# GNN preparation on one core: x asked for first, half of the normalising and the moments' sums on GpSimd, one edge step at a time

## The chip, the core and the metric

The kernel runs on one core of one Trainium2 chip. The metric is the device time of one execution in microseconds (us), and the time of a kernel is the median of several runs. Profiled executions give a span (first to last instruction) and, a little longer, the execution's own time. Engines are named as in the profile: PE is TensorE's matmul, PEld its weight load, DVE is VectorE, ACT is ScalarE, POOL is GpSimd, and SP is SyncE, which here only issues DMAs.

## What is computed

x is 6250 nodes by 256 channels; src and dst hold 100,000 edges, sorted by dst. The reference normalises x, runs three layers and a head, and adds the result to x:

```
h = relu(layernorm(x))
for l in 0..2:  h = relu((h + agg(h)) @ W1[l] + b1[l]);  h = relu(h @ W2[l] + b2[l]);  h = h @ W3[l] + b3[l]
h = relu((h + agg(h)) @ cW1 + cb1);  h = relu(h @ cW2 + cb2);  out = x + h @ cW3 + cb3
agg(h)[n] = sum of h[src[e]] over the edges e with dst[e] = n
```

## The kernel before

The nodes are 49 tiles of 128 rows. Since agg is linear, the kernel multiplies by W1 first: the table of layer 0 is relu(layernorm(x)) @ W1[0], and a later layer's W3 is folded into the next W1. Most of agg is done as dense products with a count matrix of the graph, built on the chip from the edges; for the other tiles (`gone`) rows are gathered from the table by indirect DMA.

All this runs inside `tc.manual_schedule()`: each engine's instructions stand in the order in which the program issues them, so an instruction that waits holds everything behind it on its engine. The preparation (line 1147 on) interleaves three generators, and each `next` issues a stage of one of them:

- `rows = normed(...)` (L1009) makes table 0 and its two halves in `XY` (a rounded high part, L1103, and the rest, L1108). It works on 25 pairs of tiles; step s of its loop issues, each for another pair: `out` (the product's copy from PSUM, L1092, pair s-3), `high` (L1103, s-4), `scale` (normalise and relu, L1061, pair s), `turn` (four transposes on PE, L1070, and the copy back from PSUM, L1073, s-1), `times` (eight products with W1, L1082, s-2), `moments` (statistics, L1035, s+4, and, when a group of tiles is full, four small operations on DVE and a square root on ACT, L1041 to L1047), `low` (L1108, s-4) and `keep` (the store of four tiles to the table, s-5). `settle` (L1053) makes the scale and shift that `scale` reads. x comes in groups of six tiles (`load`, four buffers), the first group in two parts.
- `looked = look(...)` (L653) treats the edges: it loads dst (`run`) and src (`srcs`), stores two rearranged copies of them in DRAM (`split_d`, `ends_d`), finds by comparing (L785 to L813: one subtraction, three Sign passes on ACT, two compares and a reduction on DVE) where each stretch of nodes begins, asks for windows of edges by indirect DMA, turns them on PE (L892) into `clT`, from which the graph is later built, and makes the lists `idx` and `rel` for the gathers (L974 to L993).
- `ahead_w = fused(...)` (L576) turns W3 (L590) and multiplies it by the next W1 (L598), once per layer, four stages each; the biases, loaded by `load_biases` (L550) and turned on PE (L567), go into the product too.

`ask(n)` (L643) issues up to n of the waiting indirect requests on POOL. Each is tied to the newest product of `times` (`after`, L632). The driver, before:

```
STAGES = (0, 1, 2, 3, 4, 5, 6, 7, 8, 9, 10, 14, 15, 16, 17, 18, 19, 20, 21, 22, 23, 24, 25, 26, 28)
for i in range(len(range(0, NT, 2)) + 5):
    if i >= 2:
        next(ahead_w, None)
    next(rows)
    ask(2)
    if i in STAGES:
        next(looked, None)
```

Ahead of this loop the driver issues, in order: the first two tiles of x; the small load of first destinations; the rest of the first group, W1 and tiles 6 to 11; dst and src; the six bias rows, the first W3 and W1; the first moments. Step 1 of the loop asks for tiles 12 to 23. After the loop the three generators are run out. The memory of the preparation's pools is then used again: the graph build's first cast (`pairs`, L1220, on ACT) takes its place, and from there on the code is that of the layers.

## Time and profile before

| what | us |
|---|---|
| median of 3 runs | 2042.28 (2041.14 to 2042.76) |
| profiled execution, its own time | 2041.49 |
| its span | 2039.3 |
| PE busy | 1985.8 |
| POOL busy | 1376.4 |
| DVE busy | 909.8 |
| ACT busy | 850.9 |
| first `pairs` cast (L1220) starts | 105.40 |

The page gives one profiled execution. The chain of waits is followed back from the last instruction to what released each step. In a timeline row stand the start, the duration, the engine, the line of the kernel, the operation with its tiles, how many, and in brackets the idle time before it with what ended it. A row of the stretches gives each engine's busy time and number of instructions in a window, then PE's granted clock (1.00 is full), the DMA engines' busy share and GB/s. A row of the groups gives busy time and the mean of one in ns. "SPq" and "ACTq" are DMA issues of those engines' queues.

### The profile page before, as it was taken

How to read it: one execution, taken by the hardware profiler on the slowest of the kernel's cores; microseconds unless marked ns; L12 is line 12 of the kernel's file. 1: busy time of each engine (PE TensorE's matmuls, PEld its weight loads, DVE VectorE, ACT ScalarE, POOL GpSimd, SP SyncE). 2: the span in 40 equal slices, each digit the busy share in tenths (PEclk: the TensorE clock that was granted, in tenths of full speed). 3: DMA queues.
4: the chain of work that ended last, by engine and by line, in shares of the span. 5: the costliest groups of instructions: out<-in, count | busy, mean ns of one | idle time of the engine just before them, and what ended most of it. 6: DMA issues, size and time to landing. Idle time of an engine off the chain costs nothing.

```text
span 2039.3 us, 32998 instructions
## 1 busy us (share of the span) xinstructions
PE 1985.8 (97%) x12075; PEld 1469.4 (72%) x12075; DVE 909.8 (45%) x2080; ACT 850.9 (42%) x1743; POOL 1376.4 (67%) x1452
## 2 busy tenths in 40 slices
PE   5999999999999999999999999999999999999997
PEld 4866766666766877777777777777777777777774
DVE  6788776777672422222333322222233432333333
ACT  5776655556565533232243323223323433233331
POOL 1557777777773577777676577777777477777774
PEclk9999999999999999999999999999999999999999
DMA  6644555555454755455556554555556555655553
GB/s 210 187 143 147 161 153 157 157 159 154 151 157 151 252 165 153 154 173 166 152 178 201 184 167 145 185 159 170 152 184 208 181 189 156 208 192 184 175 175 117
DMA packets 184774, 347.21 MB, mean 170 GB/s; under 512 B 31544, under 2 KB 119098, under 8 KB 184604
## 3 DMA queue, kind: packets, MB, share of 16 engines
q0 software_dynamic: 67440, 183.10, 31.1%
q1 hardware_dynamic: 116632, 160.07, 23.7%
q8 instruction: 96, 1.57, 0.3%
q10 hardware_dynamic: 532, 1.86, 0.3%
q14 instruction: 74, 0.61, 0.1%
HBM read 286.05 MB, written 58.87 MB: 169 GB/s over the span
## 4 chain that ended last, share of the span: by engine, by line
PE 91%; DVE 4%; DMA 2%; ACT 1%; issue 1%; POOL 0%; SPq 0%; ACTq 0%; DVEq 0%; POOLq 0%
PE agg L1945 46%; PE agg L1862 13%; PE sums L1679 11%; PE ps L1503 6%; PE ps L1440 6%; PE bp L1263 4%; PE ps L1745 1%; DVE hi L1225 1%; DVE at L1273 1%; PE bp L1082 1%; DVE lo L1225 1%; PE ps L1432 1%; PE ps L1452 1%; DMA srcs<-in_src_dram 0%; DMA xs<-in_x_dram 0%
## 5 line engine op out<-in xcount | busy, mean ns | idle before, releaser
L1618 POOL DMA_INDIRECT rows<-table,idx x1352 | 1312.3, 971 | 572.2 <-issue 217.1
L1945 PE MATMUL agg<-a,XY 128*128 128x512 f32 x4116 | 978.2, 395 | 2.0 <-DMA table<-zz 2.0
L1945 PEld LDWEIGHTS agg<-a,XY 128*128 128x128 f32 x4116 | 765.7, 188 | 192.6 <-issue 34.7
L1838 ACT CAST a<-at 128x512 fp32r<-128x512 uint8 (+1 forms) x529 | 320.8, 617 | 590.6 <-PE agg L1945 562.7
L1838 DVE CAST a<-at 128x512 fp32r<-128x512 uint8 x528 | 239.8, 456 | 480.8 <-PE agg L1945 463.9
L1862 PE MATMUL agg<-XY,a 128*128 128x512 f32 x1323 | 369.3, 410 | 1.4 <-DVE un L1874 0.7
L1862 PEld LDWEIGHTS agg<-XY,a 128*128 128x128 f32 x1323 | 230.9, 189 | 42.0 <-issue 5.0
L1679 PE MATMUL sums<-rows,hot 128*32 128x256 f32 x3724 | 242.3, 381 | 4.4 <-DMA rows<-table,idx 4.4
L1679 PEld LDWEIGHTS sums<-rows,hot 128*32 128x32 f32 x3724 | 122.4, 110 | 116.4 <-issue 29.3
L1271 ACT CAST at<-bp 128x392 uint8<-128x392 f32 x250 | 120.8, 489 | 188.2 <-PE bp L1263 187.6
L1822 ACT CAST a<-at 128x512 fp32r<-128x512 uint8 (+2 forms) x349 | 191.3, 574 | 7.8 <-PE agg L1862 7.3
L1273 DVE CAST at<-bp 128x392 uint8<-128x392 f32 x230 | 128.7, 559 | 129.5 <-PE bp L1263 129.3
L1703 DVE TENSOR_TENSOR sums<-sums,XY 128x256 f32<-128x256 f32 x85 | 36.5, 430 | 295.0 <-PE agg L1945 277.0
L1225 DVE TENSOR_TENSOR hi<-cols,pairs 128x784 bf16<-128x784 bf16 x240 | 133.8, 558 | 0.0
L1503 PE MATMUL ps<-w,h 128*128 128x256 f32 x588 | 133.5, 379 | 0.0
L1440 PE MATMUL ps<-h,w 128*128 128x512 f32 (+3 forms) x328 | 133.1, 548 | 0.3 <-ACT h L1958 0.3
L1263 PE MATMUL bp<-hi,lo 128*128 128x196 bf16 x960 | 124.4, 250 | 8.8 <-DVE hi L1225 8.1
L1263 PEld LDWEIGHTS <-lo 128*128 128x128 bf16 x960 | 70.1, 98 | 77.7 <-DVE hi L1225 29.0
L1503 PEld LDWEIGHTS ps<-w,h 128*128 128x128 f32 x588 | 111.4, 190 | 16.4
L1749 ACT ACTIVATE h<-ps,bias 128x256 f32<-128x256 f32 (+1 forms) x118 | 47.8, 461 | 155.4 <-PE ps L1745 155.4
L1225 DVE TENSOR_TENSOR lo<-lanes,pairs 128x512 bf16<-128x512 bf16 x240 | 99.2, 413 | 0.8 <-ACT pairs L1220 0.8
L1440 PEld LDWEIGHTS ps<-h,w 128*128 128x128 f32 x328 | 59.9, 189 | 54.0 <-issue 43.1
(213 smaller groups left out, 1011.3 us busy)
## 6 DMA issues: line engine op xcount, KB each, us to landing
at<-mat SPq DMA_DIRECT2D x149, 448.0 KB
mat<-at SPq DMA_DIRECT2D x30, 784.0 KB
rows<-table,idx POOLq DMA_INDIRECT x1352
table<-zz SPq DMA_DIRECT2D x71, 256.0 KB
back<-table SPq DMA_DIRECT2D x109, 128.0 KB
table<-zs SPq DMA_DIRECT2D x12, 512.0 KB
out_dram<-zz SPq DMA_DIRECT2D x23, 256.0 KB
xt<-in_x_dram SPq DMA_DIRECT2D x22, 256.0 KB
```

Of the source, the lines that this page charges most:

```text
L1225: nc.vector.tensor_tensor(o.rearrange("p q (n t) -> p q n t", t=2), values.rearrange("p (n t) -> p n t", t=2)[:, None, :, :].to_broadcast( ...
L1263: mm = nc.tensor.matmul(bp[:, m * HW:(m + 1) * HW], lo[:, q + m, :], hi[:, q + m, :], start=True, stop=True)
L1271: nc.scalar.copy(o, v)
L1273: nc.vector.tensor_copy(o, v)
L1440: mm = nc.tensor.matmul(ps[:mp, :w], weights[l][0][:, c, i * P:i * P + mp], h1[:, c, :w], start=(c == 0), stop=(c == KC - 1))
L1503: mm = nc.tensor.matmul(o, h2[0][:, c, nodes], w3[:, c, :], start=(c == 0), stop=(c == KC - 1))
L1618: got = nc.gpsimd.indirect_dma_start(out=t, out_offset=None, in_=tables[self.l][:, :], in_offset=bass.IndirectOffsetOnAxis(ap=at, axis=0),)
L1679: nc.tensor.matmul(self.sums[m * Q:(m + 1) * Q, :C], self.hot[:, c - min(rounds), m, :], self.shared[over_of[b + i]] if k == T else self.r ...
L1822: nc.scalar.copy(a[:, i * m * P:(i + 1) * m * P].rearrange("p (j d) -> p j d", j=m), counts[b][:, j:j + m, :])
L1838: cast(o, at[:, :, d:d + m * P])
L1862: mm = nc.tensor.matmul(agg, a[:, d:d + P], XY[:, j, :], start=(j == 0), stop=(j == NT - 1))
L1945: mm = nc.tensor.matmul(agg[c][:, :w], XY[:, j, o:o + P], a[:, :w], start=(at == 0 and half == 0), stop=(at == NT - 1 and half == 1))
```

## The change

- x: tiles 12 to 17 are asked for with tiles 6 to 11, ahead of dst and src; tiles 18 to 23 stay at step 1.
- Biases: no longer a tile of their own but rows in the memory of `clT`, set to zero by POOL before the loop, loaded at step 5 together with the first W3 and W1, and turned within the first fused product. The fused products start at step 10 of the loop instead of 2, and the next W1 is asked for one stage later.
- `scale`: the first tile of a pair on ACT, the second on POOL, without relu; the relu is in the turned copy. Three buffers for `h` instead of two, and `turn`, `times`, `out`, `high`, `low` and `keep` each one step later. The five operations of the moments' sums are on POOL, as are the small operations on the counts (`less` to `begin_size`).
- `out`: every second pair on ACT instead of every third, the last two on DVE, and these store at once.
- `look`: the stages are arranged anew. The comparing comes first and the rearranging of the edges is shared out over stages between its passes; the check of the order (`down`) is two stages, the last windows, the gathers' lists and the small checks change places. The loop has 31 steps instead of 30, asks for three requests a step instead of two, and gives `looked` 21 stages in it instead of 25.

The diff, cut to its core:

```diff
-    def load_biases(pool):
+    def load_biases():
...
         nc.gpsimd.memset(rows, 0.0)
-        r = 0
...
-            r += n
+        def bring():
+            r = 0
+            for ap in (b1s, cb1, b2s, b3s, cb2):
+                n, c = ap.shape if len(ap.shape) == 2 else (1, ap.shape[0])
+                flat = ap if len(ap.shape) == 2 else ap.rearrange("(o c) -> o c", o=1)
+                for c0 in range(0, max(c, P), c):
+                    nc.sync.dma_start(out=rows[r:r + n, c0:c0 + c], in_=flat)
...
-        turn()()
...
             shut()
+            if l == 0:
+                turn()()
             open_copies.append(times(KC, l, box))
-            w1 = right_of(l + 1)
             yield
             shut()
+            w1 = right_of(l + 1)
...
-        nc.vector.tensor_scalar(chunk[:R], srcs[:R], 7, None, op0=OP.arith_shift_right)
-        nc.vector.scalar_tensor_tensor(split[:R, :, 0], run[:R, :EC], float(STEP), chunk[:R],
-                                       op0=OP.mult, op1=OP.add)
-        nc.vector.scalar_tensor_tensor(split[:R, :, 1], chunk[:R], float(-P), srcs[:R],
-                                       op0=OP.mult, op1=OP.add)
-        store(split_d, split, REST)
...
-        node = pool.tile([P, GSUB, NSUB - S0], F32, name="chunk", bufs=1)
-        nc.gpsimd.iota(node, pattern=[[STEP * GD, GSUB], [STEP * 64, NSUB - S0]],
-                       base=STEP * 64 * S0, channel_multiplier=0,
-                       allow_small_or_imprecise_dtypes=True)
-        yield
-        ends = pool.tile([P, EC, 2], I32, name="split", bufs=2)
-        nc.scalar.copy(ends[:R, :, 0], run[:R, :EC])
-        yield
-        nc.scalar.copy(ends[:R, :, 1], srcs[:R])
-        store(ends_d, ends, REST + P)
-        yield
...
-        sign(0)
-        yield
-        for i, (g0, g1) in enumerate(((0, 9), (9, GSUB + 1))):
+        def compare(g0, g1):
             shape = [NSUB, g1 - g0, NEAR // FINE]
...
+        sign(0)
+        yield
+        ends = pool.tile([P, EC, 2], I32, name="split", bufs=2)
+        nc.vector.tensor_scalar(chunk[:R], srcs[:R], 7, None, op0=OP.arith_shift_right)
+        nc.vector.scalar_tensor_tensor(split[:R, :, 0], run[:R, :EC], float(STEP), chunk[:R],
+                                       op0=OP.mult, op1=OP.add)
+        nc.scalar.copy(ends[:R, :, 0], run[:R, :EC])
+        yield
+        nc.vector.scalar_tensor_tensor(split[:R, :, 1], chunk[:R], float(-P), srcs[:R],
+                                       op0=OP.mult, op1=OP.add)
+        nc.scalar.copy(ends[:R, :, 1], srcs[:R])
+        yield
+        store(split_d, split, REST)
+        compare(0, 9)
+        sign(1)
+        store(ends_d, ends, REST + P)
+        node = pool.tile([P, GSUB, NSUB - S0], F32, name="chunk", bufs=1)
+        nc.gpsimd.iota(node, pattern=[[STEP * GD, GSUB], [STEP * 64, NSUB - S0]],
+                       base=STEP * 64 * S0, channel_multiplier=0,
+                       allow_small_or_imprecise_dtypes=True)
+        yield
+        compare(9, GSUB + 1)
+        sign(2)
+        yield
...
-        nc.vector.tensor_scalar(less[:NSUB], less[:NSUB], -0.5, float(NEAR // 2), op0=OP.mult,
+        nc.gpsimd.tensor_scalar(less[:NSUB], less[:NSUB], -0.5, float(NEAR // 2), op0=OP.mult,
                                 op1=OP.add)
-        nc.vector.tensor_scalar(first[:NSUB], less[:NSUB], at[:NSUB, 0:1], None, op0=OP.add)
+        nc.gpsimd.tensor_scalar(first[:NSUB], less[:NSUB], at[:NSUB, 0:1], None, op0=OP.add)
...
-        nc.vector.tensor_tensor(more[:NSUB], both[:NSUB, 5:6], both[:NSUB, 4:5], OP.subtract)
-        nc.vector.scalar_tensor_tensor(both[:NSUB, 4:5], more[:NSUB], even[:NSUB, 0:1],
-                                       both[:NSUB, 4:5], op0=OP.mult, op1=OP.add)
+        nc.gpsimd.tensor_tensor(more[:NSUB], both[:NSUB, 5:6], both[:NSUB, 4:5], OP.subtract)
+        nc.gpsimd.tensor_scalar(more[:NSUB], more[:NSUB], even[:NSUB, 0:1], both[:NSUB, 4:5],
+                                op0=OP.mult, op1=OP.add)
+        nc.gpsimd.tensor_copy(both[:NSUB, 4:5], more[:NSUB])
...
+        down = pool.tile([P, EC], BF16, name="junk", bufs=1)
+        nc.vector.tensor_tensor(down[:R], run[:R, 1:EC + 1], run[:R, :EC], OP.is_lt)
+        yield
+        nc.vector.tensor_reduce(wrong[:R, 0:1], down[:R], axis=mybir.AxisListType.X, op=OP.max)
...
-        ask(len(asks) - NQ - parts_of[2][1])
-        yield from divided(1)
-        yield
-        down = pool.tile([P, EC], BF16, name="junk", bufs=1)
-        nc.vector.tensor_tensor(down[:R], run[:R, 1:EC + 1], run[:R, :EC], OP.is_lt)
-        nc.vector.tensor_reduce(wrong[:R, 0:1], down[:R], axis=mybir.AxisListType.X, op=OP.max)
-        yield
...
+        ask(len(asks) - NQ - parts_of[2][1])
+        yield from divided(1)
+        yield
+        ask(len(asks) - parts_of[2][1])
+        fd = pool.tile([P, NQ, P], F32, name="run", bufs=1)
+        fs = pool.tile([P, NQ, P], F32, name="near", bufs=1)
+        for q0, q1 in ((0, NQ - 1), (NQ - 1, NQ)):
+            r = gone[q0][1] * T
+            nc.vector.tensor_tensor(fd[:r, q0:q1], gds[:r, q0:q1, :, 0],
+                                    base[:r, q0:q1, None].to_broadcast([r, q1 - q0, P]),
+                                    OP.subtract)
+            nc.scalar.copy(fs[:r, q0:q1], gds[:r, q0:q1, :, 1])
+        yield
+        ask(len(asks))
+        yield from divided(2)
...
-        yield
-        ask(len(asks))
-        yield from divided(2)
-        yield
-        ask(len(asks))
-        yield
-        fd = pool.tile([P, NQ, P], F32, name="run", bufs=1)
-        fs = pool.tile([P, NQ, P], F32, name="near", bufs=1)
-        for q0, q1 in ((0, NQ - 1), (NQ - 1, NQ)):
-            r = gone[q0][1] * T
-            nc.vector.tensor_tensor(fd[:r, q0:q1], gds[:r, q0:q1, :, 0],
-                                    base[:r, q0:q1, None].to_broadcast([r, q1 - q0, P]),
-                                    OP.subtract)
-            nc.scalar.copy(fs[:r, q0:q1], gds[:r, q0:q1, :, 1])
...
-                nc.vector.tensor_tensor(apart[:, :m], v[:, :m, 1], v[:, :m, 4], OP.subtract)
-                nc.vector.tensor_tensor(both[:, :m, :], v[:, :m, 1:3], v[:, :m, 4:6], OP.add)
-                nc.vector.scalar_tensor_tensor(apart[:, :m], apart[:, :m], float(C // 4),
-                                               apart[:, :m], op0=OP.mult, op1=OP.mult)
-                nc.vector.tensor_tensor(both[:, :m, 1], both[:, :m, 1], apart[:, :m], OP.add)
+                nc.gpsimd.tensor_tensor(apart[:, :m], v[:, :m, 1], v[:, :m, 4], OP.subtract)
+                nc.gpsimd.tensor_tensor(both[:, :m, :], v[:, :m, 1:3], v[:, :m, 4:6], OP.add)
+                nc.gpsimd.tensor_tensor(apart[:, :m], apart[:, :m], apart[:, :m], OP.mult)
+                nc.gpsimd.tensor_scalar(apart[:, :m], apart[:, :m], float(C // 4), None, op0=OP.mult)
+                nc.gpsimd.tensor_tensor(both[:, :m, 1], both[:, :m, 1], apart[:, :m], OP.add)
...
         def scale(s):
             i0, n = pairs[s]
-            h[s] = pool.tile([P, 2, C], F32, name="h", bufs=2)
+            h[s] = pool.tile([P, 2, C], F32, name="h", bufs=3)
             for i in range(i0, i0 + n):
-                nc.scalar.activation(h[s][:, i - i0, :], xs[i // G * G][:, i % G, :], AF.Relu,
-                                     bias=shift[:, i:i + 1], scale=rstd[:, i:i + 1])
+                o, v = h[s][:, i - i0, :], xs[i // G * G][:, i % G, :]
+                if i - i0:
+                    nc.gpsimd.tensor_scalar(o, v, rstd[:, i:i + 1], shift[:, i:i + 1],
+                                            op0=OP.mult, op1=OP.add)
+                else:
+                    nc.scalar.activation(o, v, AF.Identity, bias=shift[:, i:i + 1],
+                                         scale=rstd[:, i:i + 1])
...
             ht[s] = pool.tile([P, KC, 2 * P], F32, name="ht", bufs=2)
-            nc.scalar.copy(ht[s][:, :, :n * P],
-                           pt.rearrange("p (c n) -> p c n", c=KC)[:, :, :n * P])
+            nc.scalar.activation(ht[s][:, :, :n * P],
+                                 pt.rearrange("p (c n) -> p c n", c=KC)[:, :, :n * P], AF.Relu)
...
             o = zs[s - s % 2][:, s % 2 * 2:s % 2 * 2 + n, :]
-            copy = nc.scalar.copy if s % 3 == 1 else nc.vector.tensor_copy
+            copy = nc.scalar.copy if s % 2 and s < len(pairs) - 2 else nc.vector.tensor_copy
             copy(o, zp.pop(s)[:, :n * C].rearrange("p (i c) -> p i c", c=C))
+            if s >= len(pairs) - 2:
+                keep(s)
...
-                rows_io(tables[0], i0, n, zs.pop(k), False)
...
         load(0, 0, HEAD)
         yield
         load(0, HEAD)
         w1 = load_w("w1_0", W1s[0], pool, nc.sync, bufs=1)
         load(G)
+        load(2 * G)
...
-        for s in range(len(pairs) + 5):
+        for s in range(len(pairs) + 6):
             if s == 1:
-                for t0 in (2 * G, 3 * G):
-                    load(t0)
+                load(3 * G)
             if s <= len(first_moments):
                 settle(s + LEAD)
             if s % (G // 2) == 0 and s and s * 2 + 3 * G < NT:
                 load(s * 2 + 3 * G)
-            for lag, f in ((3, out), (4, high), (0, scale), (1, turn), (2, times), (-LEAD, moments),
-                           (4, low), (5, keep)):
+            for lag, f in ((4, out), (5, high), (0, scale), (2, turn), (3, times), (-LEAD, moments),
...
-                elif 0 <= s - lag < len(pairs):
+                elif 0 <= s - lag < len(pairs) - 2 * (f is keep):
...
-            turn_biases, (b1, b2, b3) = load_biases(prep)
+            bring_biases, turn_biases, (b1, b2, b3) = load_biases()
             ahead_w = fused(prep, [W3s[l] for l in range(NLAYER)],
-                            [W1s[l + 1] for l in range(NLAYER - 1)] + [cW1], turn_biases, b3)
-            next(ahead_w)
+                            [W1s[l + 1] for l in range(NLAYER - 1)] + [cW1], bring_biases, turn_biases, b3)
...
-            STAGES = (0, 1, 2, 3, 4, 5, 6, 7, 8, 9, 10, 14, 15, 16, 17, 18, 19, 20, 21, 22, 23, 24, 25, 26, 28)
-            for i in range(len(range(0, NT, 2)) + 5):
-                if i >= 2:
+            STAGES = (0, 1, 5, 6, 7, 8, 9, 10, 11, 14, 15, 16, 17, 18, 19, 20, 21, 22, 23, 24, 25)
+            for i in range(len(range(0, NT, 2)) + 6):
+                if i == 5 or i >= 10:
                     next(ahead_w, None)
                 next(rows)
-                ask(2)
+                ask(3)
                 if i in STAGES:
                     next(looked, None)
```

35 lines of the change are left out of this document (15 added, 20 removed).

## The prediction

> **What bounds the kernel now.** I read the page first, its span and engine shares, then the chain of waits, the stretches and the timeline of the preparation.
>
> ```profile
> span 2039.3 us, 32998 instructions
> PE 1985.8 (97%) x12075; PEld 1469.4 (72%) x12075; DVE 909.8 (45%) x2080; ACT 850.9 (42%) x1743; POOL 1376.4 (67%) x1452
> ```
>
> PE is busy 97% of the span, and the diff touches only the preparation, the first 5%, so the question is when the preparation ends. Its end is the first cast of the graph build, at 105.40:
>
> ```profile
> 99.82 1.13 PE L1082 MATMUL bp<-w,ht 128*128 128x256 f32 x4
> 102.77 1.94 DMA table<-zs
> 105.40 0.40 ACT L1220 COPY pairs<-clT 128x64 bf16<-128x64 bf16 x2 [2.22 <-DVE sums L1773]
> ```
>
> The last product ends at 100.95, its copy is stored and lands, and 4.45 us later the casts begin. No line behind them changes, so I carry a shift of 105.40 one to one to the end of the span. The stretches of 10 us say which engine holds which part:
>
> ```profile
> 10.00:20.00 10.00, 4.43 (x14) 3.79 (x15) 5.32 (x13) 2.42 (x7) 3.42 (x18) 1.00 0.85 221
> 20.00:30.00 10.00, 7.26 (x36) 6.12 (x35) 3.46 (x13) 6.11 (x14) 0.00 (x0) 1.00 0.77 274
> 30.00:40.00 10.00, 8.66 (x46) 6.89 (x45) 7.39 (x17) 8.30 (x16) 0.00 (x0) 1.00 0.54 157
> 40.00:50.00 10.00, 5.96 (x22) 4.70 (x21) 5.95 (x11) 7.35 (x16) 0.00 (x0) 0.83 0.62 201
> 60.00:70.00 10.00, 10.00 (x59) 8.96 (x58) 6.34 (x20) 8.36 (x17) 6.40 (x6) 1.00 0.72 218
> 80.00:90.00 10.00, 8.16 (x41) 6.17 (x39) 9.45 (x35) 7.32 (x15) 6.30 (x7) 1.00 0.56 164
> ```
>
> The columns are PE, PEld, DVE, ACT, POOL busy, then clock, DMA share and GB/s. To 30 us PE starves and DMA is the busiest; from 30 to 50 ACT leads; from 60 PE is full. The first part in the chain of waits and the timeline:
>
> ```profile
> 5.35 8.31 DMA srcs<-in_src_dram
> 15.56 0.36 PE L567 MATMUL ps<-ident,brows 11*128 11x11 f32 x2 [6.59 <-DMA brows<-in_L_gnn_cb_dram]
> 22.46 0.75 DVE L1035 BATCH_NORM_STATS2 stats<-xs 128x6 f32<-128x256 f32 x2 [4.70 <-DMA xs<-in_x_dram]
> 23.60 1.09 ACT L1061 ACTIVATE h<-xs,shift,rstd 128x256 f32<-128x256 f32 x2 [3.06 <-DVE shift L1054]
> SPq L557 <- DMA xs<-in_x_dram: 2.8, 2, 2.4
> ```
>
> PE waits 6.59 us for biases, and the fourth pair (s=3) isn't scaled before 23.60, because tiles 12 to 17 were asked for behind edges, biases (whose issue waits on SP) and weights.
>
> **Front: x first.** Tiles 12 to 17 (768 KB) take the place in SP's queue that run and srcs had (781 KB), whose last bytes landed at 5.35 + 8.31 = 13.66; I let x land there. From the statistics to scaling took 23.60 − 22.46 = 1.14, and the sums now cross to POOL and back, 0.2: scaling of s=3 at 15.0, 8.6 us earlier. The biases leave this queue and PE's (to step 5, turned at 13); the edges land one transfer later, near 17.2, and are first read at step 6.
>
> **ACT-bound steps 3 to 9.** The next x (tiles 18 to 23) stands behind 781 + 768 KB, 7.0 us at 221 GB/s: 20.7. Step 5's comparison is queued on DVE behind its statistics (0.75) and settling (0.35, my estimate of its share of the 1.14), and ACT's first Sign waits for it. Rows for the steps:
>
> ```profile
> L1061 ACT ACTIVATE h<-xs,shift,rstd 128x256 f32<-128x256 f32 x49 | 26.9, 599 | 5.8 <-DVE shift L1054 4.6 <-issue 1.2
> 66.39 0.47 ACT ht L1073
> L1103 ACT CAST XY<-zs 128x1024 fp32r<-128x1024 f32 x12 | 12.6, 1051 | 0.7 <-DVE zs L1092 0.7
> L1092 ACT COPY zs<-bp 128x512 f32<-128x512 f32 x8 | 4.7, 587 | 1.7 <-PE bp L1082 1.7
> L795 ACT ACTIVATE near_i<-near,edge 98x1280 bf16<-98x1280 f32 x3 | 4.1, 1364 | 1.0 <-issue 1.0
> L795 ACT ACTIVATION_READ_ACCUMULATOR near_i<-near,edge 98x1 f32 x3 | 0.6, 194 | 0.0
> L1047 ACT ACTIVATE std<-pair,eps 128x6 f32<-128x6 f32 x7 | 2.1, 305 | 0.5 <-DVE pair L1045 0.5
> L779 ACT COPY split<-srcs 113x892 int32<-113x892 int32 x1 | 1.0, 983 | 0.0
> L785 DVE TENSOR_SCALAR near<-near_i,low 98x1280 f32<-98x1280 int32 x1 | 0.9, 886 | 0.0
> 16.52 0.35 ACTq L733 DMA_DIRECT2D split_d<-split  x1
> ```
>
> Sign can start at 20.7 + 0.75 + 0.35 + 0.89 = 22.7 and with its accumulator read (0.19) ends at 24.2. Then ACT per step, with one scaling (0.55, half the 1.09 of a pair) and one turned copy (0.47): step 6 adds a high half and an ends copy, 3.05; step 7 an out copy, an ends copy and a root (0.3), 2.88; step 8 a high half, Sign and four DMA issues, 5.0; step 9 an out copy and Sign, 3.15. That is 14.1, so step 10 begins at 38.3 and its turned copy ends at 39.3. Relu in place of copy I cost at nothing: same tile, same engine.
>
> PE's prices:
>
> ```profile
> 50.40 0.86 PE ps L598 x4
> 51.26 0.44 PE agg L1070 x4
> 51.70 1.73 PE bp L1082 x8
> 59.94 1.73 PE ps L598 x8
> 68.86 0.84 PE L892 MATMUL ps<-ident,split 98*128 98x98 f32 x6
> 55.59 0.91 PE ps L853 x14
> ```
>
> A pair is 0.44 + 1.73 = 2.17. So step 11's product, with the weights' turn (0.44) beside it, ends at 41.4.
>
> **Steps 11 to 19: the new queue on GpSimd.** POOL does half of each pair, the sums, and the edge requests, and all go in its one order. Each request is tied to the newest product; scaling of the next step is queued behind three of them, and PE's turning two steps on waits for that.
>
> ```profile
> L647 POOL DMA_INDIRECT split<-split_d,starts x16 | 16.9, 1057 | 43.7 <-PE bp L1082 37.6 <-issue 3.7 <-ACT zs L1092 2.1
> 55.05 0.97 POOL L647 DMA_INDIRECT split<-split_d,starts  x1 [0.30 <-issue]
> masks.py:199 POOL TENSOR_SCALAR_AFFINE_SELECT ident<-ident 128x128 f32<-128x128 f32 x1 | 0.3, 315 | 0.1
> L772 POOL IOTA chunk<- 128x992 f32 x1 | 1.3, 1267 | 4.3 <-DVE split L754 4.3
> L762 POOL IOTA names<- 128x4 f32 x5 | 0.5, 132 | 0.1
> 65.43 1.23 DVE L1108 TENSOR_TENSOR XY<-zs,XY 128x1024 fp32r<-128x1024 f32 x1 [2.37 <-ACT XY L1103]
> 65.90 1.60 POOL L647 DMA_INDIRECT split<-split_d,starts  x1 [0.30 <-issue]
> ```
>
> A request costs 0.97 + 0.30 = 1.27. POOL's 128x256 scaling isn't in the trace: bounds 0.32 (a select over half the elements) and 1.27 (an iota over four times as many); I take 0.5, near the first. [...] Small operations I take as 0.15 to 0.19, just over the iota's 0.13. The low half (L1108) and a request in flight together made the request 1.60, 0.63 more; three such meetings, 2.0.
>
> From 41.4: three requests 3.8, eleven small operations moved from DVE 2.1, then until scaling of pair 17 is done six scalings 3.0, fifteen requests 19.05, two groups of sums 1.5 and the meetings 2.0: 31.4, at 72.8. PE alone would be there sooner: seven pairs 15.2, weights 1.73 + 0.86 + 0.44 + 1.73 + 0.86 + 0.44 = 6.1, biases 0.36, the blocks of L853 with the two products behind them 1.2 (estimated from the 0.91) and two groups of edge turns 1.68, in all 24.5. So POOL holds PE up by 6.9 us. ACT carries 0.55 + 0.47 and half of 1.05 + 0.59 a step, with the weights' copies some 2.2; DVE, busy 6.3 of 10 us in the full stretch above, loses the sums: both stay under these.
>
> **Rest and end.** From the turn of pair 17: eight pairs 17.4, weights 2.6, edges 1.68 + 0.6, the half pair 0.95: 23.2, at 96.0. The tail was 4.45; the integer subtraction (1.06) that stood ahead of the last copy on DVE moves forward and the small checks (0.9) move behind, so 3.7: **99.7**. The last store already left beside its copy, so its move is worth nothing more.
>
> Sum: 105.4 − 99.7 = 5.7 us. The profiled execution took 2041.49 (2.2 around its span), 0.8 below the median 2042.28: 2035.8 there, 2036.6 at the median. About 0.2%, 4.1 us, is what a measurement here can tell from no change, and the forecast is only little beyond it.
>
> **What could bend a term.** The deeper pipeline (one more step) is in the 23.2; it is paid by PE idling early, which costs nothing where x is awaited. SP is moved past little: loads of tiles 12 go before edges, and w3/w1 to step 5, with readers five steps later. Identity for Relu: no row here shows it; bounds zero and a table load each way (1.28 in the row below) for nine roots on ACT, 23 us. [...]
>
> ```profile
> L677 ACT ACT_TABLE_LOAD x1 | 1.3, 1283 | 0.7 <-PEq L2059 0.7
> ```
>
> **Rivals.** *POOL does not hold PE* (chance 0.20): requests slip into PE's own stalls, or PE is late anyway. Then 41.4 + 24.5 + 23.2 + 3.7 = 92.8, gain 12.6: 2029.7. For it: requests waited on products for 37.6 us in all, POOL had 3.6 of 10 us free from 60 to 70; against it: three requests a step make 4.3 us against 2.17 to 3.9.
>
> *The gain is eaten, no change* (0.24): POOL's scaling costs the 1.27 of its far bound (six times 0.77, 4.6 us), or x does not land at 13.7 and the front's 8.6 shrinks by half: gain about 1, 2041. To this belongs a full lock: if each low half held a POOL operation for all of its 1.23 rather than 0.63, and DVE in return waited, three meetings plus the moved compare (1.07) add some 3 to 4 us; gain 2, 2040. [...]
>
> *Slower* (0.06): POOL becomes the pace of the whole stretch. Each 0.1 us of scaling costs 0.6; break-even is 0.5 + 5.7/6 = 1.45 us, and at 2.2 (beyond either bound) the time is 4.5 us longer, 2046.8. A table switch around the roots would be as bad (0.02, inside the 0.08 below).
>
> **How the numbers follow.** Forecast as summed 0.48, its own range 2033 to 2040 (scaling 0.32 to 1.0, meetings none to five), of which a fifth lies within 0.2%. Faster: 0.38 + 0.20 + a little of the third case = 0.59; same 0.33; slower 0.08. The range runs from the first rival's time less 1.7 to just past no change: 2028 to 2043.
>
> **What would show it.** Right: s=3 scaled near 15, no PE wait on brows, first Sign near 23, POOL busy without gaps from about 41 to 70 with PE's turning waiting on POOL there, the graph's first cast near 99.7. Wrong: PE full through the requests (first rival), POOL scaling above 1 us, a second table load, or statistics waiting past 16 for x.

## The result

The changed kernel takes 2056.76 us (median of 6 runs, 2054.09 to 2060.34) beside 2042.57 us for the kernel before (6 runs, 2041.14 to 2047.08): a ratio of 1.0062, 95% interval 1.005 to 1.0074. It is slower by 13 to 14 us where the forecast said 5.7 faster; the time lies outside the range given. The profiled execution took 2059.59.

The page of the changed kernel, in its first lines:

```profile
span 2057.8 us, 33027 instructions
...
PE 1999.7 (97%) x12075; PEld 1478.2 (72%) x12075; DVE 902.7 (44%) x2027; ACT 841.7 (41%) x1722; POOL 1412.4 (69%) x1537
```

PE executes the same 12075 matmuls and is "busy" 14 us longer for it (1999.7 beside 1985.8): part of the loss is not idle time but matmuls that ran slower. Where the preparation ends, and what the front did, in the timeline of ACT:

```profile
16.29 0.60 ACT L1067 ACTIVATE h<-xs,shift,rstd 128x256 f32<-128x256 f32 x1 [0.58 <-DVE shift L1055]
...
21.46 1.36 ACT L778 ACTIVATE near_i<-near,edge 98x1280 bf16<-98x1280 f32 x1
...
117.98 0.40 ACT L1227 COPY pairs<-clT 128x64 bf16<-128x64 bf16 x2 [4.16 <-DMA table<-zs]
```

The front came nearly as forecast: s=3 is scaled at 16.29 (23.60 before), the first Sign starts at 21.46 (35.29 before). Yet the first cast of `pairs` is at 117.98, 12.6 us later than the 105.40 of before. So nearly the whole loss arises between 21 and 118 us. Its stretches, with the columns as before:

```profile
30.00:40.00 10.00, 7.40 (x25) 6.11 (x26) 8.30 (x12) 8.69 (x15) 5.02 (x9) 0.66 0.94 277
40.00:50.00 10.00, 9.73 (x53) 8.04 (x51) 5.01 (x14) 6.66 (x15) 6.65 (x13) 1.00 0.89 271
50.00:60.00 10.00, 4.21 (x31) 3.11 (x29) 2.67 (x5) 2.86 (x6) 8.11 (x15) 0.96 0.27 85
60.00:70.00 10.00, 9.07 (x34) 7.50 (x34) 7.13 (x18) 3.88 (x8) 8.61 (x9) 0.70 0.33 92
70.00:80.00 10.00, 5.27 (x15) 4.29 (x16) 0.39 (x3) 4.06 (x9) 6.67 (x12) 0.66 0.61 190
```

From 50 to 80 DVE, ACT and DMA all have room, PE is busy for 18.6 of 30 us and POOL, for 23.4, leads. From 60 to 70 PE looks nearly full, but with 34 matmuls at a clock of 0.70; before, the same slice held 59 at 1.00. The view of waits, 0 to 125 us (total, times, longest):

```profile
ACT std L1048 <- POOL pair L1046: 30.8, 9, 8.1
...
DVE XY L1116 <- ACT XY L1111: 12.4, 6, 7.2
...
PE ps L601 <- ACT w L603: 7.7, 2, 5.0
...
PE ps L593 <- ACT w L603: 2.6, 1, 2.6
...
PE agg L1076 <- POOL h L1064: 1.6, 2, 1.3
```

The wait that the forecast looked for, PE's turning on POOL's half of `h`, is 1.6 us. The large one is ACT's: its square root waits 30.8 us for `pair`, the last of the sums that were moved to POOL. One such wait, POOL's timeline first:

```profile
46.26 0.97 POOL L651 DMA_INDIRECT split<-split_d,starts  x1 [0.30 <-issue]
47.27 0.20 POOL L833 TENSOR_SCALAR less<-less 98x3 f32<-98x3 f32 x1
...
50.05 0.93 POOL L853 TENSOR_SCALAR begins<-names,since,both 98x28 f32<-98x28 f32 x2
50.95 0.57 POOL L1064 TENSOR_SCALAR h<-xs,rstd,shift 128x256 f32<-128x256 f32 x1
51.70 1.11 POOL L651 DMA_INDIRECT split<-split_d,starts  x1 [0.18 <-issue]
...
55.42 0.55 POOL L1064 TENSOR_SCALAR h<-xs,rstd,shift 128x256 f32<-128x256 f32 x1
55.95 0.20 POOL L1042 TENSOR_TENSOR apart<-stats 128x6 f32<-128x6 f32 x1
...
56.91 0.20 POOL L1046 TENSOR_TENSOR pair<-pair,apart 128x6 f32<-128x6 f32 x1
```

The five sums take 1.2 us, but they stand behind eleven small operations (3.7 us), two scalings and four requests. In the same time on ACT, and then on PE:

```profile
48.49 0.60 ACT L1079 ACTIVATE ht<-agg 128x512 f32<-128x512 f32 x1 [0.73 <-PE agg L1076]
57.14 0.30 ACT L1048 ACTIVATE std<-pair,eps 128x6 f32<-128x6 f32 x1 [8.06 <-POOL pair L1046]
57.35 0.35 ACT L603 COPY w<-ps 128x256 f32<-128x256 f32 x1
57.60 1.05 ACT L1111 CAST XY<-zs 128x1024 fp32r<-128x1024 f32 x1
```

```profile
57.76 0.44 PE L593 MATMUL ps<-ident,w 128*128 128x128 f32 x2 [2.64 <-ACT w L603]
...
61.10 1.06 PE L1076 MATMUL agg<-ident,h 128*128 128x128 f32 x4
61.96 3.62 PE L1088 MATMUL bp<-w,ht 128*128 128x256 f32 x8
...
67.82 1.89 PE L1088 MATMUL bp<-w,ht 128*128 128x256 f32 x8
74.73 2.07 PE L601 MATMUL ps<-w1n,bias 128*128 128x256 f32 x4 [5.02 <-ACT w L603]
```

The root is at the head of ACT's order and ACT does nothing for 8.06 us. Behind it stand the copy of the fused weights (57.35), for which PE waits, and the high half (57.60), for which DVE waits. And when PE goes on, the eight products of a pair take 3.62 us instead of 1.89 and four turns 1.06 instead of 0.60.

### The profile page after: what moved, and what is told of

Its sections match the earlier page's. It is cut to its first block, busy times and chain, and to the rows that moved or that the text cites. A ratio compares the mean times of both kernels' runs of the same rounds, so it can differ in the third digit from the quotient of the medians.

```text
span 2057.8 us, 33027 instructions
## 1 busy us (share of the span) xinstructions
PE 1999.7 (97%) x12075; PEld 1478.2 (72%) x12075; DVE 902.7 (44%) x2027; ACT 841.7 (41%) x1722; POOL 1412.4 (69%) x1537
## 4 chain that ended last, share of the span: by engine, by line
PE 90%; DVE 4%; POOL 2%; DMA 2%; issue 1%; ACT 1%; SPq 0%; ACTq 0%; DVEq 0%; POOLq 0%
PE agg L1952 46%; PE agg L1869 13%; PE sums L1686 11%; PE ps L1447 6%; PE ps L1510 6%; PE bp L1270 4%; PE ps L1752 1%; PE bp L1088 1%; DMA rows<-table,idx 1%; DVE hi L1232 1%; DVE at L1280 1%; DVE lo L1232 1%; PE ps L1439 1%; PE ps L1459 1%; POOL rows L1625 0%
## 5 line engine op out<-in xcount | busy, mean ns | idle before, releaser
L1232 DVE TENSOR_TENSOR lo<-lanes,pairs 128x512 bf16<-128x512 bf16 x240 | 99.7, 415 | 3.8 <-ACT pairs L1227 2.5
```

What stands on the lines that cost most here:

```text
L1232: nc.vector.tensor_tensor(o.rearrange("p q (n t) -> p q n t", t=2), values.rearrange("p (n t) -> p n t", t=2)[:, None, :, :].to_broadcast( ...
```

## The theories and the experiments

**Theory A:** the root at the head of ACT's queue waits for sums on GpSimd that are queued behind requests; ACT's queue stands, and PE behind it. **Theory B**, the forecast's own step: requests on GpSimd hold PE through the scaled tiles. **The third:** neither queue, but the deeper pipeline and the new order of the edge steps.

The table has every run: ratio to the kernel before, run beside it on the same chip, with its 95% interval; what that is on 2042.5 us; and the first cast of `pairs` in the profiled execution (105.40 before).

| run | ratio (95%) | us | first cast |
|---|---|---|---|
| changed kernel | 1.0062 (1.005–1.0074) | +12.7 | 117.98 |
| a1_sums_dve | 0.9991 (0.9983–1.0) | −1.8 | 104.18 |
| a2_root_late | 1.0011 (1.0003–1.002) | +2.2 | 107.97 |
| a3_scale_act | 1.0033 (1.0023–1.0044) | +6.7 | 112.06 |
| a4_ask2 | 1.0016 (1.0006–1.0025) | +3.3 | 109.85 |
| b1_sums_pool | 1.0027 (1.0014–1.004) | +5.5 | 113.86 |
| b2_x_ahead | 0.9989 (0.998–0.9998) | −2.2 | 106.50 |
| c3_front | 0.9997 (0.9988–1.0006) | −0.6 | 106.19 |
| a6_counts_dve | 0.9977 (0.9967–0.9987) | −4.7 | 99.69 |
| a7_counts_keep | 0.9965 (0.9952–0.9977) | −7.1 | 98.50 |
| c2_all_act | 0.9949 (0.9935–0.9962) | −10.4 | 97.54 |
| c4_ask2 | 0.9937 (0.9924–0.9951) | −12.9 | 94.90 |
| d1_all_act_ask2 | 0.9944 (0.9929–0.9959) | −11.4 | 95.17 |
| c1_act_held | 1.0095 (1.0079–1.011) | +19.4 | 122.54 |
| d2_held_spread | 1.0044 (1.0029–1.006) | +9.0 | 119.10 |

Expectations in absolute time were written on a before of about 2042.5; the kernel before measured 2044.9 to 2046.7 beside these runs, so the column in us is what they are to be held against.

**a1_sums_dve**, the changed kernel with the sums on VectorE:

```diff
-                nc.gpsimd.tensor_tensor(apart[:, :m], v[:, :m, 1], v[:, :m, 4], OP.subtract)
...
+                nc.vector.tensor_tensor(apart[:, :m], v[:, :m, 1], v[:, :m, 4], OP.subtract)
...
```

> The changed kernel with one part undone: the moments' sums (L1042 to L1046) are on VectorE again, in four operations as before; all else as changed. In the changed kernel ACT waited 30.8 us in all for these sums ahead of its square roots, 8.1, 5.5 and 3.2 us of it in single waits between 49 and 93 us. Theory A (the root stands at the head of ACT's queue and waits for sums that stand on GpSimd behind edge requests, and all of ACT's copies wait behind it): the three long waits, 16.8 us, go, and some slow clock after them; GpSimd's half of the scaling then holds PE somewhat, as forecast: first cast of the graph build near 102 to 106 instead of 118, time 2040 to 2046. Theory B (GpSimd's requests hold PE through the scaled tiles, whoever does the sums): only the 1 us of each group's sums leaves GpSimd's queue, time 2052 to 2056.

−1.8 us, or 2040.7, in A's range: the whole loss goes with five operations of 0.2 us. Of the timeline of ACT:

```profile
48.59 0.30 ACT L1048 ACTIVATE std<-pair,eps 128x6 f32<-128x6 f32 x1 [0.34 <-DVE pair L1046]
64.49 0.29 ACT L1048 ACTIVATE std<-pair,eps 128x6 f32<-128x6 f32 x1
...
104.18 0.40 ACT L1227 COPY pairs<-clT 128x64 bf16<-128x64 bf16 x2 [4.15 <-DMA table<-zs]
```

The roots that stood for 8.06 and 5.50 now wait 0.34 and nothing. A holds; the third falls as the cause of the loss, since a1 keeps the deeper pipeline and the new order of the edge steps.

**a2_root_late**: the sums stay on GpSimd, the root is moved to where its result is used, about a step later.

```diff
-                nc.scalar.activation(std[:, :m], both[:, :m, 1], AF.Sqrt, bias=eps, scale=1.0 / C)
                 stds.append((s, t0, m, std, both))
...
                 _, t0, m, std, both = stds.pop(0)
+                nc.scalar.activation(std[:, :m], both[:, :m, 1], AF.Sqrt, bias=eps, scale=1.0 / C)
```

> The changed kernel with the sums still on GpSimd, but each square root issued on ACT about one step later, at the place where VectorE's reciprocal is issued. Theory A: each long wait of ACT shrinks by about a step's work (2 to 3 us), and what is queued behind the root gets done first: 5 to 9 us of the 14 come back, time 2047 to 2052. Theory B: nothing changes, 2055 to 2059.

+2.2: moving one instruction of 0.3 us in ACT's order takes back some 10 of the 13 to 14 us with nothing changed on GpSimd, more than A's 5 to 9 and nothing that B allows. Two long waits of the root remain, 4.05 and 3.65 us, and the time is 4.0 us over a1; no run shows whether it is these waits that cost them.

**a3_scale_act** (all scaling on ScalarE, sums still on GpSimd) and **a4_ask2** (two requests a step) shorten what stands ahead of the sums.

```diff
-                if i - i0:
-                    nc.gpsimd.tensor_scalar(o, v, rstd[:, i:i + 1], shift[:, i:i + 1],
-                                            op0=OP.mult, op1=OP.add)
-                else:
-                    nc.scalar.activation(o, v, AF.Identity, bias=shift[:, i:i + 1],
-                                         scale=rstd[:, i:i + 1])
+                nc.scalar.activation(o, v, AF.Identity, bias=shift[:, i:i + 1],
+                                     scale=rstd[:, i:i + 1])
```

```diff
-                ask(3)
+                ask(2)
```

> The changed kernel with another part undone: both tiles of a pair are scaled on ACT again (still without relu), the sums stay on GpSimd. Theory A: GpSimd's queue is shorter by 0.55 us a step, but the sums still stand behind three requests, and ACT has 0.55 us a step more to do: between 4 us faster and 4 us slower than the changed kernel, 2052 to 2061. Theory B: PE no longer waits for GpSimd's tiles, 7 us faster or more, below 2050.

> The changed kernel with two edge requests a step instead of three. Two requests (2.5 us) and a scaling (0.55) are about a step of PE's, so no queue should build up on GpSimd. Theory A: the sums are reached in time, the long waits of ACT shrink to about 2 us each: 7 to 12 us of the 14 come back, 2044 to 2050. Theory B expects the same sign and about 7 us, 2050. If the queue is not what hurts (a third theory: the deeper pipeline and the new order of the edge steps), no change, 2055 to 2059.

+6.7 and +3.3, or 2049.2 and 2045.8. The second lies in A's range, though the longest wait was expected near 2 us. The first lies under A's range (2052 to 2061) and inside B's (below 2050), so A's expectation for a3 missed, and by its time alone a3 would speak for B. Its trace does not: the changed kernel's PE had waited only 1.6 us for GpSimd's tiles, too little for the 6.0 us that a3 gains, while a shorter queue let the sums come sooner. The roots wait 21.3 us in a3 (longest 5.6) and 24.5 in a4 (longest 4.8) in place of 30.8 (8.1). The loss follows the longest wait and not the sum, as far as two runs can show that; a3 also gives ACT more to do. And a3 removes B's whole mechanism and keeps half of the loss.

**b1_sums_pool**: the kernel before with its sums on GpSimd, nothing else changed (the diff of a1 the other way).

> The kernel before with one part of the change alone: the moments' sums as five small GpSimd operations, two edge requests a step as before. Theory A (the square root stands in ScalarE's order and waits for sums that queue behind requests on GpSimd) makes it depend on the backlog: two requests of about 1.3 us in a step of about 4 us leave GpSimd time to drain, so the root waits 1 to 3 us in the groups that fall among the requests, and the time is 2043 to 2049, slower than before by 1 to 6 us. If the sums on GpSimd were dear by themselves, whatever is queued with them (a rival), each of the seven groups would lose its 1 us and more, and the root's wait would be as long as in the changed kernel, 5 to 8 us: 2050 or more. If the sums cost nothing without the third request and the later order, the time is within 1 us of before.

+5.5, the upper end of A's figure; its interval (+2.9 to +8.2) reaches into the rival's times, but the waits are not the rival's 5 to 8 us. The last five roots wait 1.78, 1.84, 3.12, 2.36 and 2.23 us, none near 5; two requests a step and little beside them make a short queue, and still this one edit costs some 5 us.

**c1_act_held**: a1, with the sums still on VectorE; ACT copies something unread ahead of the same three roots.

```diff
+        HOLD = {30: 17, 36: 12, 48: 7}
...
+                for _ in range(HOLD.get(t0, 0)):
+                    nc.scalar.copy(XY[:, NT - 1, :].rearrange("p (a b) -> p a b", b=P),
+                                   ident[:, None, :].to_broadcast([P, 4, P]))
                 nc.scalar.activation(std[:, :m], both[:, :m, 1], AF.Sqrt, bias=eps, scale=1.0 / C)
```

> The kernel with the sums on VectorE (a1_sums_dve, 1.8 us under before), in which ScalarE is kept busy with copies that nothing reads ahead of three square roots: 17, 12 and 7 copies of 128x512 at about 0.48 us, so about 8.1, 5.7 and 3.4 us, where the changed kernel's root waited 8.06, 5.50 and 3.22 us for GpSimd. GpSimd has no part in it. Theory A (the loss is ScalarE's queue standing still, whoever stops it, and what stands behind it) makes it as slow as the changed kernel: the first cast of the pairs at 112 to 119, 2051 to 2058, and the granted clock under 0.85 in at least two slices of 10 us between 50 and 100. The rival (the sums cost by what GpSimd does, its port and its requests, and ScalarE's stop is mostly slack): the time stays under 2049.

+19.4, beyond the expected range: a copy took 0.645 us, not 0.48, so the stops were 10.9, 7.7 and 4.4, 23 us in all. Against a1 that is 21 us lost for 23 us of stop; at that rate the three waits of the changed kernel (16.8 us) are worth 15.5, and 14.5 were lost. Its stretches, columns as before, two of a1's, and one row of c1's timeline of PE:

```profile
40.00:50.00 10.00, 7.62 (x39) 6.11 (x39) 6.66 (x21) 7.47 (x16) 7.21 (x15) 1.00 0.88 280
50.00:60.00 10.00, 6.11 (x29) 4.53 (x29) 0.92 (x1) 9.65 (x18) 8.11 (x10) 0.57 0.27 72
60.00:70.00 10.00, 8.50 (x34) 7.09 (x34) 7.22 (x23) 5.84 (x12) 7.62 (x9) 0.74 0.62 201
70.00:80.00 10.00, 3.46 (x10) 2.90 (x11) 0.72 (x4) 7.95 (x17) 3.42 (x5) 0.60 0.16 45
```

```profile
50.00:60.00 10.00, 7.66 (x37) 6.24 (x38) 4.54 (x15) 2.62 (x6) 8.34 (x10) 0.68 0.36 113
...
70.00:80.00 10.00, 8.48 (x47) 7.24 (x48) 8.37 (x28) 5.12 (x12) 8.20 (x11) 1.00 0.83 291
```

```profile
76.54 2.07 PE L601 MATMUL ps<-w1n,bias 128*128 128x256 f32 x4 [7.07 <-ACT w L603]
```

The stops were put into ACT's queue alone, and TensorE's granted clock fell with the second of them: 0.60 from 70 to 80 us, where a1 has 1.00, around a wait of 7.07 us for ACT's copy of the weights. The 0.57 from 50 to 60 is not the first stop's alone: a1 has 0.68 there, and in both kernels the slow products begin behind a wait for GpSimd's scaled tile (2.41 us in c1, 2.89 in a1). A's mechanism is shown with no sum on GpSimd.

**d2_held_spread**: the same 36 copies, five or six ahead of each of seven roots.

```diff
-        HOLD = {30: 17, 36: 12, 48: 7}
+        HOLD = {12: 5, 18: 5, 24: 5, 30: 5, 36: 5, 42: 5, 48: 6}
```

> The kernel of c1_act_held with the same 36 copies on ScalarE, five or six ahead of each of seven square roots instead of 17, 12 and 7 ahead of three. A copy took 0.645 us there, so seven stops of 3.2 to 3.9 us stand for three of 10.9, 7.7 and 4.4 us, 23 us in both. If the loss goes by the sum of the stops, the time is that of c1_act_held within 3 us, 2058 to 2063 on a before of 2042.5. If short stops are partly covered by what the pipeline has ahead, and the clock stays up because TensorE's gaps are short, it is 2046 to 2056 and no slice of 10 us is below a clock of 0.8.

+9.0, the second outcome in time: 10.8 us over a1 for 23 us of stop, half of what c1's three stops cost. Length and place changed together here, since four of the seven stops stand ahead of other roots than c1's, so it is likely, and not shown, that short stops are the cheaper ones. Its clock did fall, to 0.83, 0.73 and 0.66 in single slices, after gaps of 2.5 to 3.7 us on PE, so that half of the expectation was wrong. (Its profiled execution, 2061.28, was the longest of its six; the 119.10 in the table goes with that one.)

**b2_x_ahead** and **c3_front**: the kernel before with x asked for first; then with the whole front.

```diff
         load(G)
+        load(2 * G)
...
-                for t0 in (2 * G, 3 * G):
-                    load(t0)
+                load(3 * G)
```

```diff
         w3, w1 = left_of(0), right_of(0)
+        bring()
...
-        turn()()
...
+            if l == 0:
+                turn()()
             open_copies.append(times(KC, l, box))
```

> The kernel before with one part of the change alone: the third group of x (tiles 12 to 17) is loaded ahead of the edges instead of behind the biases and weights. The prediction's front says that the scaling of pair 3, at 23.60 us in the kernel before, is late by this load alone and comes near 16 us. If what is gained at the front carries through, the first cast of the pairs comes 4 to 7 us earlier than 105.40 and the time is 2035 to 2040. The rival: the edges land later for it and the edge steps set the middle of the preparation, so that the front's gain is given back there and the time is 2040 to 2044.

> The kernel before with the front of the change in full and nothing else: the third group of x ahead of the edges, the biases' DMAs behind the first weights, and the turn of the biases three steps later. In b2_x_ahead TensorE stood 10.2 us for the biases' rows, to 19.17, in place of the later wait for x. If that wait was all that ate the front's gain, the first product comes near 12 to 13 us instead of 16.8, the first cast of the pairs at 99 to 102 and the time is 2036 to 2040 on a before of 2042.5. If the edge steps hold the middle, the cast stays at 103 to 106 and the time is 2040 to 2043.

−2.2 (at the edge of what can be told) and −0.6 (nothing), both as their rivals had it. PE's timeline of the first and of the second:

```profile
19.17 0.36 PE L567 MATMUL ps<-ident,brows 11*128 11x11 f32 x2 [10.20 <-DMA brows<-in_L_gnn_cb_dram]
```

```profile
11.42 3.62 PE L1086 MATMUL bp<-w,ht 128*128 128x256 f32 x8
18.89 0.96 PE L593 MATMUL ps<-ident,w 128*128 128x128 f32 x4 [3.85 <-DMA w<-in_L_gnn_W3s_dram]
```

Whatever comes first in SP's queue, PE's order waits for what has become last: for biases to 19.17, then, with these moved, for W3 at 18.89, although the first product began at 11.42 instead of 16.76. What is left of the front goes to the edge steps, which c3 leaves in their old order: the first Sign starts at 35.09, beside 35.29 before, and PE turns the fifth pair at 32.72, beside 32.65. The change also starts the fused products later and takes the comparing first (its first Sign is at 21.46); no run tells which of the two keeps the front's gain.

**a6_counts_dve**, **a7_counts_keep**, **c2_all_act**, **c4_ask2**, **d1_all_act_ask2**: taking the rest off GpSimd's queue. a6 is a1 with the eleven small operations of the counts on VectorE, as before. a7 adds an order in which the store of pairs 20 and 21 goes first in its step:

```diff
-            for lag, f in ((4, out), (5, high), (0, scale), (2, turn), (3, times), (-LEAD, moments),
-                           (5, low), (6, keep)):
+            for lag, f in ((6, keep), (4, out), (5, high), (0, scale), (2, turn), (3, times),
+                           (-LEAD, moments), (5, low)):
```

c2 is a7 with the diff of a3, c4 is a7 with the diff of a4, d1 has both.

> The changed kernel with the moments' sums and also the eleven small operations of the counts back on VectorE (the 3.7 us on GpSimd from 47.27 to 50.98 in the changed kernel). With the sums alone on VectorE the first cast of the pairs came at 104.18 and one wait of 3.23 us for GpSimd's scaled tile stood at 52.28, behind those small operations. Theory A, extended: what GpSimd's queue holds up is each short operation on which an in-order engine waits, so this wait goes, the cast comes at 100 to 102, and the time is 2038 to 2042. If the path is set elsewhere (the end of the preparation: stores, last copies), the time stays within 1.5 us of 2043.6.

> The kernel of a6_counts_dve, and the store of the tiles of pairs 20 and 21 is issued first in its step, so ahead of the stores of the last two pairs instead of behind them. Of the 5.9 us from the last product to the first cast of the pairs some 1.5 to 3 us are taken by stores that are issued in one row at the end; if their order is what costs, the time is 1.5 to 3 us below that of a6_counts_dve, 2036 to 2040, and the kernel is faster than both. If the last store waits for its own tile and not for the queue, the two agree within 1 us.

> The kernel of a7_counts_keep (sums and counts on VectorE, stores reordered), with both tiles of a pair scaled on ScalarE: GpSimd keeps only the requests. It asks what half of the normalising on GpSimd is worth once no short operation waits there. ScalarE takes 24 more scalings of about 0.50 us in a stretch of some 90 us in which it is busy to about seven tenths, and TensorE loses its 5.7 us of waits for GpSimd's tile. If ScalarE has the room: within 1.5 us of a7 or below it, 2033 to 2037 on a before of 2042.5. If ScalarE becomes the bound between 20 and 50 us, where it is already at 7 to 10 of 10 us: 2 to 5 us above a7.

> The kernel of a7_counts_keep with two edge requests a step instead of three. TensorE's waits for GpSimd's scaled tile there are 5.7 us in six; they stand behind three requests of about 1.3 us. If those waits are on the path, two requests a step take 1.5 to 4 us off: 2032 to 2034 on a before of 2042.5. If the later requests make the last edge steps late by as much, the time is within 1.5 us of a7.

> The kernel of c2_all_act (sums and counts on VectorE, both tiles scaled on ScalarE, stores reordered) with two requests a step instead of three, so that nothing waits behind a request on GpSimd but the requests. If three requests cost by the scaled tiles that queue behind them (the theory), two make no difference here: the time is within 1.5 us of c2_all_act's, 2031 to 2034 on a before of 2042.5. If requests cost by themselves (their pace, the descriptors, what they take from VectorE and the edge steps), two a step gain as they did in c4_ask2, 2 to 5 us: 2026 to 2030.

a6: −4.7, or 2037.8, a little under the expected range, and the cast 4.5 us earlier than in a1; the two intervals just overlap. The wait it was to remove, in a1's timeline of the weight loads, is a turn whose second tile stood behind the counts on GpSimd (in a6 the longest wait of this kind is 2.5 us):

```profile
52.28 0.31 PEld L1076 LDWEIGHTS agg<-ident,h 128*128 128x128 f32 x3 [3.23 <-POOL h L1064]
```

a7: −7.1, and the time from the last product to the cast falls as expected, since the last store lands in 2.65 instead of 3.04 us and is issued sooner; the two kernels' intervals overlap, so the 2.4 us between them in the table is not settled. c2 came to 2032.1, no slower than a7 (intervals overlap): ScalarE had the room for all of the scaling. In c4 the row that theory B is about, of a7 and of c4:

```profile
PE agg L1075 <- POOL h L1063: 5.7, 6, 2.1
```

```profile
PE agg L1075 <- POOL h L1063: 0.9, 2, 0.7
```

c4 is 5.8 us faster than a7 (intervals apart), more than the expected 4 and more than these 4.8 us of wait: B's mechanism is real, once A's no longer hides it. d1 against c2, with no tile on GpSimd, gains nothing from two requests that these runs can tell (−11.4 beside −10.4, intervals overlap almost wholly): here the requests cost through what is queued behind them, not by themselves. And c4 against d1: with two requests a step, half of the normalising on GpSimd is worth nothing that these runs can tell. All five lie below both kernels, with intervals below 1; c4 is 0.63% (0.49 to 0.76%) under the kernel before.

## Why the prediction was wrong

**The step that failed** is in "Steps 11 to 19: the new queue on GpSimd": "two groups of sums 1.5". The sums were priced as POOL's time and followed to the scaled tiles only. Who waits for a sum was not asked. It is a root in ACT's order (L1048), with the weights' copies, the high halves and the turned copies behind it; before, DVE gave the sums with little waiting (2.34 us at most after 10 us), so there the root's place cost little. Even "both stay under these" was right for ACT as a share of busy time (5.57 of 10 us in the mean from 10 to 130 us) and of no use, since ACT stood, idle, for 30.8 us behind its roots. That a producer's queue stops an in-order consumer is the slower rival that should have been written; the one that was (scaling on POOL above 1.45 us) did not happen: in the stretch from 41 to 79 us one scaling took 0.82 us in the mean.

Two marks of the forecast, in the changed kernel's timeline of PE:

```profile
40.43 1.89 PE L1088 MATMUL bp<-w,ht 128*128 128x256 f32 x8
...
84.62 0.60 PE L1076 MATMUL agg<-ident,h 128*128 128x128 f32 x4
```

Step 11's product ends at 42.32 (41.4 forecast), pair 17 is turned at 84.62 (72.8), the last product ends at 112.10 (96.0) and the cast comes at 117.98 (99.7). So of the 18.3 us by which the cast is late, 0.9 arise up to step 11, 10.9 in steps 11 to 19, 4.3 from there to the last product, and 2.2 in the tail. POOL had scaled pair 17 by 78.60, 6.0 us before PE turned it: there it is not POOL's scaling that holds PE.

**No term for the clock.** Every matmul was priced from rows at a granted clock of 1.00. In the changed kernel the clock fell after gaps of PE (0.70 from 60 to 70 us and 0.66 from 70 to 80, where the kernel before has 1.00), and from 55 to 97 us PE had 12.8 us of single waits over 2.4 (2.64, 2.45, 5.02, 2.73) and, summed over the rows that took longer than the same rows at full clock, an estimated 6 to 7 us of slow matmuls behind them (3.62 and 2.96 for 1.89, 2.07 and 2.08 for 1.13, three turns 1.06 for 0.60). The slowest eight products of that stretch took 1.9 times the usual (3.62 for 1.89). In these runs the length of a single gap did not tell whether slow products follow: they followed a gap of 2.52 (d2, at 72.18), and gaps of 2.58 (d2, at 86.07), 2.74 (before, at 26.35) and 3.1 (c4, ahead of a product before 30 us) left the clock full, 1.00 in their stretches of 10 us.

**Front:** near in time (16.29 for 15.0; first Sign 21.46 for 22.7; no wait of PE for the bias rows). Most of the 1.3 us is the sums' way over POOL, taken as 0.2, which no row of before shows, and in fact 1.2, while the root waited 2.74: the cost that failed later, here still small. And c3 shows that a product begun 5.3 us earlier was worth nothing alone.

**POOL's prices:** scaling 0.55 for 0.5, undisturbed requests 1.28 apart for 1.27, sums 1.2 a group for 0.75, the eleven small operations 3.7 for 2.1. Meetings with DVE were under-counted: from 41 to 78 us two requests took 1.93 and 1.71 and two scalings 1.26 and 1.40, in all 3.3 us over their undisturbed times, where 2.0 was forecast.

**"POOL holds PE up by 6.9 us":** 1.6 us in the changed kernel, where ACT's stops gave POOL the time; 5.7 in a7, where they are gone. The size was near and lay under another wait.

**Tail:** 3.7 forecast, 5.9 measured (last product's end at 112.10, cast at 117.98), where "its move is worth nothing more" was said of the last store. SP's queue and the chain:

```profile
112.46 0.91 SPq L534 DMA_DIRECT2D table<-zs  x2
113.49 2.22 SPq L539 DMA_DIRECT2D table<-zs  x2
```

```profile
111.75 1.03 DVE zs L1098 x2
...
114.51 3.06 DMA table<-zs
```

Three stores issue in one row, because the last pairs' now go ahead of an earlier one, and the last copies stand on DVE behind a low half that itself waits for ACT. a7 takes back 1.5 us of it in the profiles (94.13 to 98.50, against 93.82 to 99.69 in a6).

**"One to one to the end":** 12.6 us at the first cast became 14.2 by the third (128.60 for 114.44) and stayed so. The late cast left PE a gap, and the graph's first products ran slowly (0.88 for 0.50); PE's timeline:

```profile
119.22 0.50 PE L1270 MATMUL bp<-hi,lo 128*128 128x196 bf16 x4 [3.73 <-DVE hi L1232]
...
122.76 0.88 PE L1270 MATMUL bp<-hi,lo 128*128 128x196 bf16 x4
```

**Identity for Relu** was taken to cost no table load, which no row of before shows; the changed kernel's whole trace has one load (1.28 us, at 0.73), as that of before has.

Open: the profiled execution is 18.1 us longer than that of before while the medians are 14.2 apart; the rest arises almost wholly beyond 1500 us in that execution, and no experiment was made on it.

## What to carry to other kernels

When an operation moves to another engine, price not its time but what its consumer's engine does until it comes: an in-order engine that reaches an early wait stops everything behind it, and an operation of 0.2 us behind a queue can cost as much as the queue (here one root waited 8.06 us for sums of 0.2 us each, and ACT did nothing in that time). Put short producers on an engine whose queue is short, or put the consumer late in its order (a2 won back 10 us with one moved line). A queue that is long for good reasons, here the requests, should carry nothing that anyone waits for soon; and take a TensorE gap of the lengths seen here, 2.5 us and more, as possibly dearer than itself, since the clock fell after many of them (after 2.52 us in d2 four products took 2.07 us in place of 1.13, after 5.02 in the changed kernel as well).

## What was not expected of the hardware

- TensorE's granted clock fell after many gaps from 2.5 us on (2.52 in d2), not after all (3.1 in c4), and eight products then took up to 3.78 us in place of 1.89 (at 32.60 in the changed kernel, after a gap of 2.91).
- GpSimd's work took longer where it met VectorE's L1116, an operation on two tiles (`zs` and `XY`): scaling took 1.50 us (a1) where it takes 0.55, the first of the sums 1.04 (changed kernel, at 37.92) where it takes 0.20, and a request 1.93 (at 44.02) where it takes 0.97. Timelines of GpSimd and VectorE in a1:

```profile
50.73 1.50 POOL L1064 TENSOR_SCALAR h<-xs,rstd,shift 128x256 f32<-128x256 f32 x1
```

```profile
50.59 1.21 DVE L1116 TENSOR_TENSOR XY<-zs,XY 128x1024 fp32r<-128x1024 f32 x1
```

VectorE's operation, which began 0.14 us earlier, kept its length in this pair (1.21 us; the median of ten in the changed kernel is 1.22), and GpSimd's ended 0.43 us after it, near its own undisturbed length of 0.55: from these numbers it looks blocked until then, and not slowed. An operation of 0.2 us met the same: the first of the sums, begun at 37.92, ended at 38.96, 0.06 us after the L1116 that VectorE had begun at 37.69.
